# The last chunk of a Mamba block: where its input and its norm's offset are added, and where GpSimd makes the next block's tap matrices

## The chip, the cores and the metric

The kernel runs on one NeuronCore of a Trainium2 chip. The metric is the device time of one execution in microseconds (us); times are the median of the runs shown. The engines are TensorE (PE in the profile, its weight load PEld), VectorE (DVE), ScalarE (ACT), GpSimd (POOL), and SyncE (SP), which here only issues DMAs.

## The reference

The whole network has four layers on an image tensor `x` of 2 x 256 channels x 32 x 32. The change lies in layer 0 and at its border to layer 1. Layer 0 is two Mamba blocks, each with a layer norm and a residual; the second runs over flipped channels, and the input `x` of the network is added to what comes out:

```python
def mamba_block(x, in_w, in_b, conv_w, conv_b, xproj_w, dt_w, dt_b, A_log, Dp, out_w, out_b):
    u = x.reshape(b, L, c)                                  # L = 1024 tokens, c = 256
    xs, res = jnp.split(u @ in_w + in_b, 2, axis=-1)        # 512 inner channels each
    xs = silu(causal_conv4(xs, conv_w) + conv_b)            # per channel, 4 taps
    dt, Bm, Cm = jnp.split(xs @ xproj_w, [16, 32], axis=-1)
    delta = softplus(dt @ dt_w + dt_b)
    A = -jnp.exp(A_log)
    dA  = jnp.exp(delta[..., None] * A)                     # 16 states
    dBu = delta[..., None] * Bm[:, :, None, :] * xs[..., None]
    # over tokens: h = dA * h + dBu ;  y = sum over states of h * C
    y = (ys + xs * Dp) * silu(res)
    return y @ out_w + out_b

xt = xt + layernorm(mamba_block(xt, m1...), ln1_w, ln1_b)
xt = flip(xt)
xt = xt + layernorm(mamba_block(xt, m2...), ln2_w, ln2_b)
# layer 0:  x = x + flip(xt);   layer 1: a dilated 7x7 convolution of x gives attention weights, ...
```

Layers 2 and 3 (attention and experts) follow and are not touched.

## The kernel before

**Tiling.** The activations `x` lie in SBUF as [128 channels, 2 channel chunks, 2 images, 1024 tokens], and `xt` is the same tile seen as [128, 2, 2048]. The Mamba work is cut into eight units: two blocks (`m1`, `m2`) times four chunks of 512 tokens (`TC`). Chunks 0 and 1 are image 0, chunks 2 and 3 are image 1. `xt` is updated in place.

**Three parts of a unit.** `front` makes the projections, the convolution and `delta`, `du`. `scan` runs 16 states; for each state n it loads a row of B to all partitions (`m_b`, line 457), multiplies it with `du` on GpSimd in two halves (the *products*, line 461), makes `exp(delta * A)` on ScalarE (line 468), scans on VectorE in four pieces (line 472), transposes on TensorE (line 440) and accumulates `y` on VectorE (line 449, `scalar_tensor_tensor`, from PSUM). `back` computes the gate, the skip term, the output projection (lines 524 and 528), the norm (`norm_rows`, lines 160 to 168), transposes back (line 179), and then, for each of the two channel chunks `cc`, updates `xt`.

**The update of `xt` in `back`.** Line 540 (ScalarE) makes `r = ps * ln_w + ln_b` from the transposed norm, line 543 (GpSimd) adds `r` to `xt`, and for the second block lines 547 and 548 load the network's input into a tile `m_x` by an SP DMA and add it on GpSimd. The tiles of `r` and of `m_x` share the tag `"r"`, which has three buffers.

**The order.** `layer0` weaves the parts together: `scan` has 63 slots, one at each scan piece, and `paced(63, steps)` calls the steps of other generators in given slots. A tuple `(generator, many, first, end)` spreads `many` steps over the slots `first` to `end`. While unit u is scanned, the front of unit u + 1 and the back of unit u - 1 run in its slots. State n covers slots 4n - 1 to 4n + 2. The tile framework then sets the order in each engine's queue: it takes instructions by the order in which they are written, but lets one go ahead of another that, by its own estimate, isn't ready. [...]

**The tap matrices.** The convolution runs on TensorE with 16 diagonal matrices per block, each the identity scaled by a column of weights on GpSimd (`diagonals`, line 269). Those of `m2` go into the buffer that those of `m1` have held until the last convolution of `m1`, so they are made in unit 2, in slots 26 to 38.

**The last unit.** There, the slots also hold the convolution of layer 1 for the first two row blocks of image 0 (`early`). Five steps of the unit's own `back` (four gate matmuls and the `Silu`) are in its slots; all the rest of it comes after the scan, woven with the convolution of the third row block:

```python
        acc = {2: taps.bank(ps_ht.tile([P, TC], F32, tag="ht", name="early_acc2"))}
        both(taps.convolve(0, pair, acc), done[0], 3)
        taps.read(acc, lg)
```

Then the pools of layer 0 are closed, and `layer1` opens its own in the same memory. Its first work is the loads of the tap pairs (`pair`, line 747, SP), a clearing of the fourth one's second half and of `band` (lines 744 and 852, GpSimd), and `turn`, which copies image 0 on GpSimd (line 863) and transposes it (line 864). Its convolution (line 769, `acc`) then keeps TensorE in work.

Of the kernel before, what the change touches and what calls it, by code (L numbers as in the profile page):

```python
# [10 lines left out]
F32 = mybir.dt.float32  # L11
# [3 lines left out]
ALU = mybir.AluOpType  # L15
# [4 lines left out]
P = 128  # L20
NB = 2
HW = 1024
# [3 lines left out]
NCC = C // P  # L26
NT = T // P
TC = 512
# [3 lines left out]
NDC = DI // P  # L32
# [201 lines left out]
class Mamba:  # L234
# [180 lines left out]
    def scan(self, j, before, between, start=False):  # L415

        net, nc, m, scanp = self.net, self.net.nc, self.m, self.scanp
        xs, bd, ct, delta, du = self.chunks[j]
        state, first = self.state, self.first(j)
        ya = self.two.tile([P, TPC, DI], F32, tag="ya", name=f"{m}_ya_{j}")
        yb = self.one.tile([P, TPC, DI], F32, tag="yb", name=f"{m}_yb_{j}")
        self.chunks[j] = xs, ya, yb
        G = 2
        half = [P, G, TC]

        def keep(n, hs):  # L430
            for g, h in enumerate(hs):
                nc.scalar.copy(state[:, n, g * G : (g + 1) * G], h[:, :, TC - 1])

        def rest(n, hs):


            for i in range(TPC):
                ps = self.ps_ht.tile([P, DI], F32, tag="ht", name=f"{m}_ht_{j}_{n}_{i}")
                for dc in range(NDC):
                    nc.tensor.transpose(  # L440
                        ps[:, dc * P : (dc + 1) * P], hs[dc // G][:, dc % G, i * P : (i + 1) * P],
                        net.ident,
                    )
                yield
                c = ct[:, i, n : n + 1]
                if n in (0, self.ASIDE):
                    nc.scalar.activation((yb if n else ya)[:, i, :], ps, AF.Copy, scale=c)
                else:
                    nc.vector.scalar_tensor_tensor(  # L449
                        ya[:, i, :], ps, c, ya[:, i, :], ALU.mult, ALU.add  # L450
                    )
                if i == 0 and first:
                    keep(n, hs)

        for n in range(NS):
            b = scanp.tile([P, TC], F32, tag="b", name=f"{m}_b_{j}_{n}", bufs=4)
            nc.sync.dma_start(b, bd[n].partition_broadcast(P))
            hs = []
            for g in range(NDC // G):
                h = scanp.tile(half, F32, tag="h", name=f"{m}_h_{j}_{n}_{g}", bufs=6)  # L460
                (nc.vector if start and n == 0 else nc.gpsimd).tensor_mul(  # L461
                    h, du[:, g * G : (g + 1) * G, :], b.unsqueeze(1).to_broadcast(half)
                )
                hs.append(h)
            for dc in range(NDC):
                da = self.ps_da.tile([P, TC], F32, tag="da", name=f"{m}_da_{j}_{n}_{dc}")
                i = dc * NS + n
                nc.scalar.activation(  # L468
                    da, delta[:, dc, :], AF.Exp, scale=self.aneg[:, i : i + 1]
                )  # L470
                h = hs[dc // G][:, dc % G, :]
                nc.vector.tensor_tensor_scan(  # L472
                    h, da, h, 0.0 if first else state[:, n, dc : dc + 1], ALU.mult, ALU.add
                )


                next(before, None)
                if n or dc:
                    next(between, None)
            before = chain(before, rest(n, hs))  # L480
        for _ in between:
            pass
        return before

    def back(self, j):

        net, nc, m, xt = self.net, self.net.nc, self.m, self.xt
        y, *sums = self.chunks.pop(j)
        tok = slice(j * TC, (j + 1) * TC)
        gate = self.one.tile([P, NDC, TC], F32, tag="gate", name=f"{m}_gate_{j}")  # L490
        for dc in range(NDC):
            ps = self.ps_mm.tile([P, TC], F32, tag="mm", name=f"{m}_g_{j}_{dc}")
            for kc in range(NCC):
                nc.tensor.matmul(  # L494
                    ps, lhsT=self.gate_sb[:, kc, dc * P : (dc + 1) * P], rhs=xt[:, kc, tok],
                    start=(kc == 0), stop=(kc == NCC - 1),
                )
            nc.scalar.activation(  # L498
                gate[:, dc, :], ps, AF.Identity, bias=net.col(f"{m}_in_b", NDC + dc)
            )  # L500
            yield
        nc.scalar.activation(gate, gate, AF.Silu)
        yield

        for dc in range(NDC):
            ps = self.ps_mm.tile([P, TC], F32, tag="mm", name=f"{m}_y_{j}_{dc}")
            nc.tensor.matmul(
                ps, lhsT=self.skip[:, dc, :], rhs=y[:, dc, :], start=True, stop=False
            )
            for k, ya in enumerate(sums):  # L510
                for i in range(TPC):
                    nc.tensor.matmul(
                        ps[:, i * P : (i + 1) * P], lhsT=ya[:, i, dc * P : (dc + 1) * P],
                        rhs=net.ident, start=False, stop=(k == 1 and i == TPC - 1),
                    )
            nc.vector.tensor_mul(y[:, dc, :], ps, gate[:, dc, :])
            yield
        o = self.one.tile([P, TPC, C], F32, tag="o", name=f"{m}_o_{j}")
        found = []
        for i in range(TPC):  # L520
            if i % 2 == 0:
                ps = self.ps_mm.tile([P, TC], F32, tag="mm", name=f"{m}_out_{j}_{i}")
            a = ps[:, i % 2 * C : (i % 2 + 1) * C]
            nc.tensor.matmul(
                a, lhsT=net.ones_row, rhs=self.out_b, start=True, stop=False
            )
            for dc in range(NDC):
                nc.tensor.matmul(
                    a, lhsT=y[:, dc, i * P : (i + 1) * P], rhs=self.out_sb[:, dc, :],
                    start=False, stop=(dc == NDC - 1),  # L530
                )
            found.append(a)
            yield
        tiles = [o[:, i, :] for i in range(TPC)]
        net.norm_rows(tiles, found, nc.scalar)
        yield
        for cc in range(NCC):
            ps = net.transposed(self.ps_mm, tiles, cc, "mm")
            r = self.one.tile([P, TC], F32, tag="r", name=f"{m}_r_{j}_{cc}", bufs=3)
            nc.scalar.activation(  # L540
                r, ps, AF.Identity, scale=net.col(f"{m}_ln_w", cc), bias=net.col(f"{m}_ln_b", cc)
            )
            nc.gpsimd.tensor_add(xt[:, cc, tok], xt[:, cc, tok], r)
            if self.x is not None:
                x = self.one.tile([P, TC], F32, tag="r", name=f"{m}_x_{j}_{cc}", bufs=3)
                at = j % (HW // TC) * TC
                nc.sync.dma_start(x, self.x[j // (HW // TC), cc, :, at : at + TC])
                nc.gpsimd.tensor_add(xt[:, cc, tok], xt[:, cc, tok], x)
            yield
# [25 lines left out]
def layer0(net, x, x_dram, m1, m2, load_image, taps, conv_dram, lg):  # L575
# [4 lines left out]
    tc, nc = net.tc, net.nc  # L580
    with (
# [10 lines left out]
        xt = x.rearrange("p c b t -> p c (b t)")  # L592
        pools = (wpool, one, two, scanp, dram, ps_mm, ps_da, ps_ht)
        blocks = [
            Mamba(net, "m1", pools, xt, None, *m1), Mamba(net, "m2", pools, xt, x_dram, *m2)
        ]
# [8 lines left out]
        for m, r in zip(blocks, rows):  # L605
            m.out_b = r
        norm.image(0)
        units = [(m, j) for m in blocks for j in range(NCH)]
        norm.image(1)
        for _ in units[0][0].front(0, alone=True):  # L610
# [3 lines left out]
        for u, (m, j) in enumerate(units):  # L614
            steps = [(b, Mamba.GATED, 0, 35) for b in done]
# [4 lines left out]
                fronts.append(a.front(k))  # L620
            if u == NCH - 2:

                steps.append((blocks[1].diagonals(), NDC * 4, 26, 38))
            rest = m.load_rest() if u and j == 0 else iter(())
            steps += [(f, Mamba.HEAD, 0, 38) for f in fronts]
            steps += [(rest, 1, 37, 38)]
# [2 lines left out]
            if u + 1 < len(units):  # L629
                n = 9 if u else 12  # L630
                steps += [(islice(aside, n), n, 40, 63)]
            else:
# [16 lines left out]
                def early():  # L649
                    for k in range(2):  # L650
                        a = ps_acc.tile([P, TC], F32, tag="acc", name=f"early_acc{k}")
                        acc = {k: taps.bank(a)}
                        yield from taps.convolve(0, pair, acc)
                        taps.read(acc, lg)

                steps += [(early(), 112, 3, 63)]
            own = m.back(j)
            if u + 1 == len(units):

                steps += [(islice(own, 5), 5, 44, 58)]  # L660
            before = m.scan(j, before, paced(63, steps), u == 0)
            done = [own]
        for _ in before:
# [1086 lines left out]
```

## Time and profile before

| what | value |
|---|---|
| runs | 2171.8, 2173.26, 2174.47 us; median 2173.26 us |
| profiled execution, its own time | 2172.59 us |
| its span in the trace | 2170.9 us |
| what lies around the span | 1.69 us |
| PE / PEld busy | 1889.3 us (87%) / 1345.8 us (62%) |
| DVE / ACT / POOL busy | 1402.7 us (65%) / 959.9 us (44%) / 1027.6 us (47%) |
| DVE in 100 to 1000 us | 86.6 to 96.5 us busy of each 100 |
| PE in 1000 to 1200 us | 92.22 and 97.00 us busy of 100 |
| GpSimd products, line 461 | 254 of 2364 ns |
| VectorE scans, line 472 | 512, of 1268 ns with a carried state and 1208 ns without |
| VectorE accumulation from PSUM, line 449 | 448 of 732 ns |
| GpSimd adds of 128 x 512, lines 543 and 548 | 16 of 1268 ns, 8 of 1269 ns |
| GpSimd scalings to tap matrices of 128 x 128, line 269 | 32 of 627 ns |

The time of a group is the sum over its instructions; an engine that is busy for a large share of the whole need not bound every stage. For this change two short stretches matter: around 330 us, where unit 2 is scanned, and 1087 to 1105 us, where layer 0 ends and layer 1 begins.

### The profile page before, as it was taken

To read this page: it belongs to the slowest core of one execution; us is meant where nothing else is said; L and a number is where in the kernel's file an instruction comes from. 1 tells how busy PE (TensorE), PEld (TensorE's weight loads), DVE (VectorE), ACT (ScalarE), POOL (GpSimd) and SP (SyncE) were. 2 spreads that over 40 slices of the span, in tenths; PEclk is the share of its full clock that TensorE was granted. 3 is DMA by queue.
4 is the path that set the end of the run, shared out by engine and by line. 5 is a ranking of instruction groups with operands and counts; after the bars stand their busy time and mean duration, and the time that the engine had idled before them with its cause. 6 is when DMAs were issued, how large, how long until landed. Compare 5 with 4: busy or idle time off the path is not lost.

```text
span 2170.9 us, 27318 instructions
## 1 busy us (share of the span) xinstructions
PE 1889.3 (87%) x9652; PEld 1345.8 (62%) x9652; DVE 1402.7 (65%) x2210; ACT 959.9 (44%) x1611; POOL 1027.6 (47%) x726
## 2 busy tenths in 40 slices
PE   6888798888989879799989989949999699859996
PEld 2364555556555645455656556539999467649995
DVE  6999997999999999897405575652222544442223
ACT  4676776767777767653213454411010132301111
POOL 3796887959698695964225420012332000023331
PEclk8969988897989889899999999969999799979997
DMA  2121121111212111310030100028999200059998
GB/s 107 45 69 40 40 67 35 53 40 45 63 48 60 35 48 34 86 40 20 5 64 1 49 15 10 20 86 304 323 332 333 83 10 10 20 208 320 334 330 294
DMA packets 90499, 223.87 MB, mean 103 GB/s; under 512 B 35467, under 2 KB 51728, under 8 KB 79732
## 3 DMA queue, kind: packets, MB, share of 16 engines
q1 hardware_dynamic: 77636, 198.29, 27.2%
q0 software_dynamic: 7728, 19.15, 3.0%
q10 hardware_dynamic: 4992, 4.59, 0.7%
q8 instruction: 81, 1.33, 0.3%
q14 instruction: 62, 0.51, 0.1%
HBM read 204.60 MB, written 19.37 MB: 103 GB/s over the span
## 4 chain that ended last, share of the span: by engine, by line
PE 32%; DVE 22%; issue 19%; POOL 12%; ACT 9%; DMA 5%; POOLq 0%; SPq 0%; ACTq 0%; DVEq 0%
DVE m_h L472 11%; DVE m_ya L449 5%; PE acc L769 3%; POOL x L1527 3%; POOL l_yd L1577 3%; PE m_ht L440 3%; PE av L1283 3%; POOL m_h L461 3%; PE early_acc L769 2%; PE sc L1257 2%; ACT m_da L468 2%; DMA l_yd<-y,target 2%; PE h L1106 2%; PE w L1115 1%; PE m_xd_ps L351 1%
## 5 line engine op out<-in xcount | busy, mean ns | idle before, releaser
L461 POOL TENSOR_TENSOR m_h<-m_du,m_b 128x1024 f32<-128x1024 f32 x254 | 594.4, 2364 | 227.6 <-PE m_ht L440 126.8
L440 PE MATMUL m_ht<-ident,m_h 128*128 128x128 f32 x2048 | 360.2, 306 | 107.2 <-DVE m_ya L449 78.4
L440 PEld LDWEIGHTS m_ht<-ident,m_h 128*128 128x128 f32 x2048 | 266.2, 156 | 299.0 <-issue 105.2
L468 ACT ACTIVATE m_da<-m_delta,m_aneg 128x512 f32<-128x512 f32 x512 | 349.0, 690 | 219.7 <-DVE m_h L472 218.8
L1527 POOL DMA_INDIRECT x<-l_zd,source x82 | 84.5, 1031 | 569.9 <-DVE source L1472 215.3
L449 DVE SCALAR_TENSOR_TENSOR m_ya<-m_ht,m_ct,m_ya 128x512 f32<-128x512 f32 x448 | 319.3, 732 | 29.2 <-PE m_ht L440 27.8
L472 DVE TENSOR_TENSOR_SCAN m_h<-m_da,m_state,m_h 128x512 f32<-128x512 f32 x256 | 316.8, 1268 | 26.9 <-POOL m_h L461 20.7
L472 DVE TENSOR_TENSOR_SCAN m_h<-m_da,m_h 128x512 f32<-128x512 f32 x256 | 302.8, 1208 | 25.3 <-ACT m_da L468 15.2
L1557 PEld LDWEIGHTS h<-xts,we 128*128 128x128 f32 x2528 | 298.3, 194 | 6.8 <-issue 2.9
L1557 PE MATMUL h<-xts,we 128*128 128x128 f32 x2528 | 299.4, 277 | 1.9 <-issue 1.5
L1564 DVE TENSOR_TENSOR hid<-hid,h 128x512 f32<-128x512 f32 x79 | 54.3, 687 | 255.5 <-PE h L1557 252.0
L1563 ACT ACTIVATE hid<-h 128x512 f32<-128x512 f32 x79 | 47.2, 597 | 381.7 <-issue 299.3
L1571 PE MATMUL o<-we,hid 128*128 128x256 f32 x632 | 150.4, 380 | 2.2 <-DVE y L1576 1.6
L1577 POOL DMA_INDIRECT l_yd<-y,target x79 | 79.0, 1000 | 142.7 <-DVE y L1576 136.4
L1571 PEld LDWEIGHTS o<-we,hid 128*128 128x128 f32 x632 | 113.7, 190 | 15.7 <-DVE y L1576 2.8
L336 PE MATMUL m_conv<-m_pre,m_taps 128*128 128x512 f32 x240 | 114.6, 596 | 6.8 <-ACT m_gate L498 5.6
L769 PE MATMUL early_acc<-x,early 128*98 128x448 f32 (+24 forms) x308 | 100.5, 453 | 0.0
L769 PE MATMUL acc<-x,pair 128*98 128x416 f32 (+21 forms) x308 | 94.0, 452 | 0.0
L1576 DVE COPY y<-o 128x256 f32<-128x256 f32 x79 | 33.6, 425 | 69.3 <-PE o L1571 69.3
L309 PE MATMUL m_in<-x,m_in_sb 128*128 128x512 f32 x128 | 67.7, 653 | 7.6 <-ACT m_pre L313 5.2
L769 PEld LDWEIGHTS acc<-x,pair 128*98 128x98 f32 x308 | 47.6, 167 | 39.1 <-issue 33.6
L494 PE MATMUL m_g<-x,m_gate_sb 128*128 128x512 f32 x128 | 66.5, 633 | 3.9 <-ACT m_o L168 2.1
(318 smaller groups left out, 2849.2 us busy)
## 6 DMA issues: line engine op xcount, KB each, us to landing
we<-in_l_experts_dram SPq DMA_DIRECT2D x82, 1536.0 KB
m_b<-m_bd SPq DMA_DIRECT2D x128, 256.0 KB
w<-in_l_w_dram SPq DMA_DIRECT2D x21, 256.0 KB
l_zd<-l_z SPq DMA_DIRECT2D x7, 512.0 KB
l_yl<-l_yd SPq DMA_DIRECT2D x10, 256.0 KB
l_yl<-l_yd ACTq DMA_DIRECT2D x10, 256.0 KB
early<-taps SPq DMA_DIRECT2D x7, 343.0 KB
pair<-taps SPq DMA_DIRECT2D x7, 343.0 KB
```

The lines of the kernel that those rows point to most:

```text
L309: nc.tensor.matmul(ps, lhsT=self.in_sb[:, kc, mc * P : (mc + 1) * P], rhs=self.xt[:, kc, tok], start=(kc == 0), stop=(kc == NCC - 1),)
L336: nc.tensor.matmul(ps, lhsT=self.taps[:, dc * 4 + k, :], rhs=pre[:, dc, k : k + TC], start=(k == 0), stop=(k == 3),)
L440: nc.tensor.transpose(ps[:, dc * P : (dc + 1) * P], hs[dc // G][:, dc % G, i * P : (i + 1) * P], net.ident,)
L449: nc.vector.scalar_tensor_tensor(ya[:, i, :], ps, c, ya[:, i, :], ALU.mult, ALU.add)
L461: (nc.vector if start and n == 0 else nc.gpsimd).tensor_mul(h, du[:, g * G : (g + 1) * G, :], b.unsqueeze(1).to_broadcast(half))
L468: nc.scalar.activation(da, delta[:, dc, :], AF.Exp, scale=self.aneg[:, i : i + 1])
L472: nc.vector.tensor_tensor_scan(h, da, h, 0.0 if first else state[:, n, dc : dc + 1], ALU.mult, ALU.add)
L769: nc.tensor.matmul(a[:, lo - 16 * k : hi - 16 * k, co : co + n], lhsT=lhsT, rhs=self.x[:, kc, b, lo - r0 : hi - r0, ci : ci + n], start=(u ...
L1527: nc.gpsimd.indirect_dma_start(out=x, out_offset=None, in_=zd[:, :], in_offset=bass.IndirectOffsetOnAxis(ap=source[:, g : g + 1], axis=0), ...
L1557: nc.tensor.matmul(ps[:, at], lhsT=w12[:, s, kc, at], rhs=xt[:, kc * P : (kc + 1) * P], start=(kc == 0), stop=(kc == NCC - 1),)
L1571: nc.tensor.matmul(ps[:, :C], lhsT=ht[:, mc * P : (mc + 1) * P], rhs=w[:, 8 + mc, :], start=(mc == 0), stop=(mc == NHC - 1),)
L1577: nc.gpsimd.indirect_dma_start(out=yd[g], out_offset=bass.IndirectOffsetOnAxis(ap=target[:, g : g + 1], axis=0), in_=y, in_offset=None, bo ...
```

## The change

Three edits. (1) Each scaling that makes a tap matrix of `m2` is traced inside `tc.issue_after(...)`, which puts it in GpSimd's queue behind the last product traced so far (`self.product`, set in `scan`); they are spread from slot 22 rather than 26. (2) In the last unit, two new steps follow the `Silu` of the gate, one for each channel chunk: the input is loaded, the norm's offset `ln_b` is added to it on GpSimd, and the sum is added to `xt` on GpSimd. They are within the scan: the own steps in its slots are now seven over slots 44 to 62, where they were five over 44 to 58. (3) At the end of the last unit, one VectorE instruction for each channel chunk, `ps * ln_w + xt` from PSUM, stands in place of the ScalarE activation, the two GpSimd adds and the load.

```diff
@@ scan
-                (nc.vector if start and n == 0 else nc.gpsimd).tensor_mul(
+                made = (nc.vector if start and n == 0 else nc.gpsimd).tensor_mul(
                     h, du[:, g * G : (g + 1) * G, :], b.unsqueeze(1).to_broadcast(half)
                 )
                 hs.append(h)
+            self.product = made
@@ back
-    def back(self, j):
+    def back(self, j, last=False):
...
         nc.scalar.activation(gate, gate, AF.Silu)
         yield
+        if last:
+            for cc in range(NCC):
+                x = self.one.tile([P, TC], F32, tag="r", name=f"{m}_x_{j}_{cc}", bufs=3)
+                at = j % (HW // TC) * TC
+                nc.sync.dma_start(x, self.x[j // (HW // TC), cc, :, at : at + TC])
+                nc.gpsimd.tensor_scalar_add(x, x, net.col(f"{m}_ln_b", cc))
+                nc.gpsimd.tensor_add(xt[:, cc, tok], xt[:, cc, tok], x)
+                yield
...
         for cc in range(NCC):
             ps = net.transposed(self.ps_mm, tiles, cc, "mm")
+            if last:
+                nc.vector.scalar_tensor_tensor(
+                    xt[:, cc, tok], ps, net.col(f"{m}_ln_w", cc), xt[:, cc, tok],
+                    ALU.mult, ALU.add,
+                )
+                yield
+                continue
             r = self.one.tile([P, TC], F32, tag="r", name=f"{m}_r_{j}_{cc}", bufs=3)
@@ layer0
+        def behind(m, steps):
+            while True:
+                with tc.issue_after(m.product.ins):
+                    if next(steps, steps) is steps:
+                        return
+                yield
...
-                steps.append((blocks[1].diagonals(), NDC * 4, 26, 38))
+                steps.append((behind(m, blocks[1].diagonals()), NDC * 4, 22, 38))
...
-            own = m.back(j)
+            own = m.back(j, u + 1 == len(units))
             if u + 1 == len(units):
-                steps += [(islice(own, 5), 5, 44, 58)]
+                steps += [(islice(own, 7), 7, 44, 62)]
```

## The prediction

> **What bounds the kernel now.** I read the page first, then windows of 100 us, the chain of waits around the two places that the diff touches, and the timeline of each engine there. The page's rows of slices (54.3 us each) show two regimes in layer 0, which ends in slice 21:
>
> ```profile
> span 2170.9 us, 27318 instructions
> PE   6888798888989879799989989949999699859996
> DVE  6999997999999999897405575652222544442223
> ```
>
> VectorE stands at 9 up to about 1000 us, so the scans bound units 0 to 6; from there PE is at 9 and VectorE falls to 4, so the last unit and the convolution after it are PE's. A stall of VectorE before 1000 us, and a hole in PE after it, each cost what they last.
>
> The hole is at the border to layer 1. The chain of waits there (start, us, what):
>
> ```profile
> 1090.28 0.91 ACT m_o L168 x2
> 1091.19 1.93 issue
> 1093.11 0.79 ACT m_r L540
> 1093.97 1.27 POOL x L543
> 1095.26 2.59 DMA m_x<-in_x_dram
> 1097.99 1.27 POOL x L548
> 1099.31 0.68 POOL pair L744
> ```
>
> After the norm there is a row of ScalarE, GpSimd, a load that had to wait for its buffer (three under tag "r"), and GpSimd again. The timeline of the same place shows what else is late, and what is held by it:
>
> ```profile
> 1094.45 0.34 ACT L788 ACTIVATE lg<-early_acc,taps_bias 98x96 f32<-98x96 f32 x1
> 1094.82 0.32 DVE L786 TENSOR_SCALAR lg<-early_acc,taps_bias 98x96 f32<-98x96 f32 x1 [5.60 <-ACT lg L788]
> 1099.27 10.55 SPq L747 DMA_DIRECT2D pair<-taps  x7
> ```
>
> The convolution's last read ends at 1095.14. Layer 1 starts on SP, VectorE and GpSimd together at 1099.3, when the last add to `xt` (to 1099.25) lets layer 0's memory go. PE has no work from 1094.3 to 1101.1. The windows there (length, PE, PEld, DVE, ACT, POOL busy, granted clock, DMA):
>
> ```profile
> 1094.30:1101.10 6.80, 0.00 (x0) 0.00 (x0) 1.83 (x11) 0.49 (x2) 6.43 (x9) 0.79 0.20 51
> 1101.10:1104.70 3.60, 2.88 (x9) 1.48 (x10) 0.00 (x0) 1.28 (x4) 2.17 (x9) 0.50 1.24 212
> 1104.70:1108.90 4.20, 4.20 (x7) 1.66 (x8) 0.00 (x0) 0.21 (x1) 0.45 (x2) 0.55 1.32 191
> 1108.90:1120.00 11.10, 11.10 (x31) 4.75 (x30) 0.00 (x0) 0.00 (x0) 0.00 (x0) 1.00 0.51 74
> ```
>
> The hole also costs clock: PE returns at half speed and has it back at about 1108.9.
>
> The other place is unit 2, GpSimd's and VectorE's timelines:
>
> ```profile
> 324.64 4.67 POOL L461 TENSOR_TENSOR m_h<-m_du,m_b 128x1024 f32<-128x1024 f32 x2 [2.53 <-issue]
> 329.29 9.29 POOL L269 TENSOR_SCALAR m_taps<-ident,cols_sb 128x128 f32<-128x128 f32 x16
> 338.55 4.66 POOL L461 TENSOR_TENSOR m_h<-m_du,m_b 128x1024 f32<-128x1024 f32 x2
> 340.93 2.34 DVE L472 TENSOR_TENSOR_SCAN m_h<-m_da,m_h 128x512 f32<-128x512 f32 x2 [4.84 <-POOL m_h L461]
> ```
>
> The 16 scalings, written one to a slot, run in one burst, since all become ready with the buffer. The next product waits behind them, and VectorE stands 4.84 us, the longest single wait on a product in 100 to 1000 us.
>
> [...] 0.50 and 0.55 after 6.8 us of idleness; a PE wait of 2.06 us at 1033 left the clock at 1.00, one of 3.13 us at 344 is followed by 0.79 in 341 to 352. [...] the same operation in line 449 takes 0.732 us, which I use. [...] no line before scales or shifts 512 elements by a column on GpSimd.
>
> **Part 1, tap matrices behind products.** Nothing is removed; 16 scalings of 0.58 us (9.29 / 16) move. Slot s belongs to state (s + 1) // 4, so slots 22 to 37 put one behind state 5's product, four each behind those of 6, 7 and 8, three behind state 9's. Products come every 7.2 to 8 us (309.59, 317.43, 324.64) and take 4.66, which leaves 2.5 to 3.3 us; four scalings take 2.32, five 2.9. They fit, but barely. The product that stood at 338.55 could then run at 324.64 + 7.9 = 332.5 or behind five scalings at 332.2, with its first half ready at 334.9; VectorE wants it at 336.09. So the wait of 4.84 us goes. Late next is ScalarE: it is in `Silu` and table loads from 332.58 to 337.27, so the second scan of that state can't start before 337.96, 0.7 us after the first ends. Gain at most 4.84 - 0.7 = 4.1. Each later batch can push its product by up to 0.4 us. PE was 9.89 of 12 us busy in that stretch and worked off other things in the wait, which it must now do beside the transposes. Bounds: a gain of 4.8, and a loss of about 2 if the new order in the queues adds a wait like the 3.13 us on PE at 344. I take 3.0. The taps are needed in unit 3, so their lateness is free; no DMA is moved.
>
> **Part 2, the input and offset within the scan.** Added: two loads on SP, two shifts and two adds on GpSimd. An add is 1.27 us. [...] I take 1.6. Sum 2 x 2.9 = 5.7 us, at most 7.3. The cover is GpSimd in the last unit:
>
> ```profile
> 1043.69 4.68 POOL L461 TENSOR_TENSOR m_h<-m_du,m_b 128x1024 f32<-128x1024 f32 x2 [10.68 <-PE m_ht L440]
> 1053.99 1.27 POOL L548 TENSOR_TENSOR x<-x,m_x 128x512 f32<-128x512 f32 x1
> 1087.34 0.24 POOL L125 IOTA iota<- 128x128 f32 x1 [32.08 <-PE m_out L528]
> ```
>
> It waits 10.68 us ahead of the last product and 32 us behind the last add. The adds to `xt` must wait for the gate matmuls (done at 1043.3), so they fall just before, or behind, the last product. On SP the loads stand with the previous chunk's two, and behind them come only small loads at 1087 and layer 1's pairs. One more tenant of tag "r" makes the previous chunk's second load wait for one add more (1050.9 rather than 1049.6), and with the chain's 2.6 us it lands at 1053.5, still ahead of its add at 1053.99. Cost 0; 0.9 us if an add goes just ahead of the last product. Without the cover it would be 5.7.
>
> **Part 3, one VectorE step.** Removed behind the transposes: two activations (1.45 us), four adds (2 x 1.27 + 2 x 1.26) and the wait for a buffer and a load. Added: 2 x 0.73 on VectorE, which is idle there. The transposes end at 1093.0 and 1093.5, so the two steps end by about 1094.6. Late next is the convolution's read, 1095.14, unchanged because PE runs the convolution to 1094.3 whatever stands there. Layer 0's memory goes at 1095.2 in place of 1099.3: **4.1 us**. All that follows (tap pairs 343 KB each, clearing, copies, transposes) hangs on that release, and PE is full from 1104.7 to 1212, so it moves as one. If VectorE's queue has the read ahead of the two steps, they end at 1096.6 and 2.6 remains.
>
> PE's hole becomes 1094.3 to 1097.0, 2.7 us, between the 2.06 that kept the clock and the 3.13 that lost it. Four wide matmuls at 0.85 rather than 0.43 us, and a few short ones, are worth up to 2 us; I take 0.5.
>
> **Sum.** 3.0 + 4.1 + 0.5 = 7.6 us off the profiled 2172.59 (span 2170.9 and 1.69 around it) is 2165.0; the median shown is 0.67 above that execution, so **2165.6**. A measurement can tell about 0.2% (4.3 us) from no change, that is 2168.9 and 2177.6.
>
> **Rivals.**
> *A, both gains* (56 in 100): 2161 to 2168. For it: both waits are in the chain.
> *B, the tail alone* (24): the burst goes, but VectorE then waits for PE or ScalarE, or the new order in the queues puts a like wait elsewhere in units 2 to 6. VectorE already waited there 20.7 us for ScalarE and 17.4 for PE in 100 to 1000. 2173.26 - 4.1 - 0.5 = 2168.7, from 2167 to 2171: on the bound, half of it faster.
> *C, little of either* (10): VectorE's steps come behind the read (2.6), part 1 loses 2: 2172.7. Also here: `issue_after` leaves the burst whole, because the buffer comes free after the later products.
> *D, slower* (10): the new adds stand ahead of the last product in GpSimd's queue. The second's load is on SP behind the previous chunk's second, which waits for an add to end at 1050.9; with its own 2.6 us and the buffer's wait it lands by about 1056, and a shift and an add later the product runs at 1059, not at 1043.7. VectorE wanted it at 1046, so 15 us are lost, less 4.6 at the end and 0 to 3 in unit 2: 2181 to 2184. It decides from a delay of 12 us on. Against it: state 15's product is written ahead of the second step, in slot 59 against 60.
>
> The range takes in A and B and most of C: 2160 to 2173. Faster: 0.53 of A, 0.13 of B, some of the rest: 0.67. Slower: D and a larger mishap of order, 0.11. Same: 0.22.
>
> **What would show it.** Right: scalings in groups of four or five between products around 325 to 355, no wait near 4.8 us; in the last unit shifts and adds between 1040 and 1060 or in the gap behind; `pair` loads some 0.1 us behind the read of the last bank; PE's hole 2.7 us. Wrong: scalings still in a burst or products starting later than their buffers allow; VectorE's steps behind the read; `pair` issued more than 1 us behind it; the last product later against the scan than now.

## The result and the profile after

The changed kernel takes 2166.99 us (median of 20 runs) beside 2175.45 us (20 runs) of the kernel before on the same chip: a ratio of 0.9959 [0.9949, 0.9969], some 9 us faster, interval 6.7 to 11.1. In later runs, which had after and before side by side again, it was 0.9942 [0.9919, 0.9964]. The forecast was 7.6 us less than before, 2165.6 us; the kernel before took 2.2 us more in these 20 runs than in the three that the forecast started from.

The page of after, its first line and the two rows of slices that the prediction read:

```profile
span 2165.4 us, 27316 instructions
PE   6888899897989889799999899949999699859996
DVE  6999999999999999897314575652222544432223
```

VectorE's row has a 9 in the seventh slice (from 325 us on), where a 7 stood before. For a size the rows are too coarse. I measured between landmarks instead, instructions that both kernels have: the start of a given GpSimd product (line 461; they are numbered from 0 here, two for most states, so that product 70 opens state 4 of unit 2 and product 96 state 1 of unit 3), and the first matmul of layer 1's convolution.

| stretch | before | after | after once more |
|---|---|---|---|
| start to product 70 (unit 2, ahead of the scalings) | 309.6 | 312.1 | 309.8 |
| product 70 to 96 (rest of unit 2, into unit 3) | 112.88 | 104.28 | 104.28 |
| product 96 to 246 (units 3 to 6) | 581.4 | 581.8 | 581.4 |
| product 246 to 252 (last unit, states 12 to 14) | 39.80 | 41.49 | 41.50 |
| product 252 to the first `acc` of layer 1 | 61.2 | 56.9 | 56.9 |

The change sits in the second, fourth and fifth row: -8.6, +1.7 and -4.3, together -11.2 us. The first row moved by 2.5 us with the same instructions, and layers 1 to 3 of the profiled after are another 2.8 us longer with the same work; so its span fell by 5.5 us only (2170.9 to 2165.4), that of its second execution by 9.2 (2161.7). A single execution of this kernel doesn't tell 3 us.

**Unit 2.** GpSimd's and VectorE's timelines of after (start, us, instruction, count, and the idle time ahead of it with what ended it):

```profile
327.18 4.67 POOL L461 TENSOR_TENSOR m_h<-m_du,m_b 128x1024 f32<-128x1024 f32 x2 [2.53 <-issue]
331.83 2.92 POOL L269 TENSOR_SCALAR m_taps<-ident,cols_sb 128x128 f32<-128x128 f32 x5
335.02 4.67 POOL L461 TENSOR_TENSOR m_h<-m_du,m_b 128x1024 f32<-128x1024 f32 x2 [0.27 <-issue]
339.67 2.33 POOL L269 TENSOR_SCALAR m_taps<-ident,cols_sb 128x128 f32<-128x128 f32 x4
345.99 4.67 POOL L461 TENSOR_TENSOR m_h<-m_du,m_b 128x1024 f32<-128x1024 f32 x2 [3.99 <-issue]
...
338.55 2.32 DVE L473 TENSOR_TENSOR_SCAN m_h<-m_da,m_h 128x512 f32<-128x512 f32 x2
```

The scalings stand in groups of five, four, four and three behind the products of states 6 to 9; the one that was written behind state 5 came with those of state 6. The product behind five of them starts 7.84 us after the one before it, where the burst had made that 13.9 us. The last line is the pair of scans that had waited 4.84 us; it runs without a wait, and both scans back to back.

VectorE's waits over the whole stretch, first before, then after (engine, tile and line, whom it waited for: us in total, times, the longest):

```profile
DVE m_h L472 <- POOL m_h L461: 6.1, 2, 4.8
DVE m_h L472 <- ACT m_da L468: 4.0, 5, 1.8
DVE m_ya L449 <- PE m_ht L440: 3.9, 5, 1.4
DVE m_xs L516 <- PE m_y L512: 0.7, 1, 0.7
```

```profile
DVE m_h L473 <- ACT m_da L469: 3.6, 5, 1.3
DVE m_ya L449 <- PE m_ht L440: 1.9, 4, 1.1
DVE m_h L473 <- POOL m_h L461: 1.1, 2, 0.6
```

VectorE is busy 97.76 us of this stretch before and 97.58 after: its work is the same, and the stretch is that work plus its waits. These fell from 14.7 to 6.6 us, 8.1 of the 8.6: 5.0 by GpSimd, 2.7 by TensorE, 0.4 by ScalarE. (Each wait is booked under whatever ended it last.)

**The border.** The timeline of after:

```profile
1089.09 1.41 DVE L550 SCALAR_TENSOR_TENSOR x<-mm_t,cols_sb,x 128x512 f32<-128x512 f32 x2 [3.85 <-PE mm_t L179]
1089.64 0.77 POOL L878 MEMSET band<- 128x384 f32 x2 [4.78 <-PE mm_t L179]
1090.45 10.68 SPq L773 DMA_DIRECT2D pair<-taps  x7
1090.72 0.32 DVE L812 TENSOR_SCALAR lg<-early_acc,taps_bias 98x96 f32<-98x96 f32 x1 [0.23 <-ACT lg L814]
...
1096.64 9.82 PE L795 MATMUL acc<-x,pair 128*98 128x512 f32 x19
```

The pair loads go out when the second VectorE step ends, and ahead of the read of the last bank (1090.72 to 1091.04). From the last product to these loads it was 55.58 us before and is 50.74 now: 4.8 us earlier. Windows of after (length, PE, PEld, DVE, ACT, POOL busy, granted clock, DMA share, GB/s):

```profile
1090.30:1091.35 1.05, 0.02 (x2) 0.01 (x1) 0.82 (x5) 0.34 (x1) 1.05 (x4) 1.00 0.03 8
1091.35:1094.35 3.00, 2.37 (x9) 1.13 (x9) 1.04 (x8) 1.25 (x4) 2.24 (x9) 1.00 0.96 178
1094.35:1096.60 2.25, 2.09 (x6) 1.06 (x7) 0.00 (x0) 0.98 (x3) 1.39 (x6) 0.52 1.28 199
1096.60:1101.50 4.90, 4.90 (x7) 1.77 (x7) 0.00 (x0) 0.37 (x1) 0.56 (x2) 0.52 1.32 191
```

TensorE's hole is 1.05 us. Then come transposes in turn with GpSimd's copies (GpSimd is busy 2.24 of 3.00 us, and each waits for the other), 14 of them ahead of `acc` where 9 stood there before. The clock falls all the same, to 0.52 from 1094.35 to 1101.5: 7.15 us, where it was 7.8 us at 0.50 and 0.55.

**The shifts and adds in the scan**, GpSimd's timeline of the last unit:

```profile
1039.71 4.68 POOL L461 TENSOR_TENSOR m_h<-m_du,m_b 128x1024 f32<-128x1024 f32 x2 [12.39 <-PE m_ht L440]
...
1047.49 1.58 POOL L511 TENSOR_SCALAR m_x<-m_x,cols_sb 128x512 f32<-128x512 f32 x1
1049.15 1.27 POOL L512 TENSOR_TENSOR x<-x,m_x 128x512 f32<-128x512 f32 x1
...
1083.37 0.24 POOL L125 IOTA iota<- 128x128 f32 x1 [27.42 <-PE m_out L538]
```

Both, and the second pair at 1053.03 and 1054.68, lie behind the last product; 27.42 us of idle time are still left.

### The profile page after: what moved, and what is told of

Read it like the earlier page. It is cut to its first block, busy times and chain, and to the rows that moved or that the text cites. A ratio compares the mean times of both kernels' runs of the same rounds, so it can differ in the third digit from the quotient of the medians.

```text
span 2165.4 us, 27316 instructions
## 1 busy us (share of the span) xinstructions
PE 1890.4 (87%) x9652; PEld 1343.7 (62%) x9652; DVE 1403.3 (65%) x2212; ACT 957.8 (44%) x1609; POOL 1028.0 (47%) x726
## 4 chain that ended last, share of the span: by engine, by line
PE 30%; issue 17%; DVE 14%; POOL 10%; ACT 7%; DMA 4%; POOLq 0%; ACTq 0%; DVEq 0%
DVE m_h L473 7%; PE acc L795 3%; POOL x L1553 3%; POOL l_yd L1603 3%; DVE m_ya L449 3%; PE av L1309 3%; PE sc L1283 2%; DMA l_yd<-y,target 2%; PE early_acc L795 2%; PE h L1132 2%; PE m_ht L440 2%; ACT m_da L469 2%; POOL m_h L461 2%; PE w L1141 1%; DMA x<-l_zd,source 1%
## 5 line engine op out<-in xcount | busy, mean ns | idle before, releaser
L1553 POOL DMA_INDIRECT x<-l_zd,source x82 | 84.5, 1030 | 571.5 <-DVE source L1498 217.0
```

Of the source, the lines that this page charges most:

```text
L1553: nc.gpsimd.indirect_dma_start(out=x, out_offset=None, in_=zd[:, :], in_offset=bass.IndirectOffsetOnAxis(ap=source[:, g : g + 1], axis=0), ...
```

## The experiments

My theory: the scalings' burst holds VectorE in unit 2, and its split frees it; at the border the release of layer 0's memory moves ahead; the added GpSimd work is covered. The rivals: unit 2's gain comes from elsewhere, or is a matter of single executions; one half of the tail alone is enough; the cover of the added work is thin.

### Each part alone

`e1_taps_only` is after with the last unit's steps as before (`m.back(j)`, five own steps in slots 44 to 58). `e2_tail_only` is after with the scalings as before:

```diff
-                steps.append((behind(m, blocks[1].diagonals()), NDC * 4, 22, 38))
+                steps.append((blocks[1].diagonals(), NDC * 4, 26, 38))
```

> Part 1 alone: the scalings go behind the products, the end of layer 0 is as before. Theory T1 (the burst costs its wait of 4.8 us on VectorE, and what that wait drags along in unit 2: TensorE stuck 3.1 us behind the copy of xd, and then at half clock): 4 to 7 us faster, ratio 0.997 to 0.998; no product wait above 2.5 us, and the stretch from the product before the scalings to the end of unit 2 is shorter by that amount. Theory T2 (the tail makes the whole gain of 8.5 us; VectorE's wait comes back as waits for TensorE or ScalarE): 0 to 1 us, ratio 0.9995 to 1.000.

> Parts 2 and 3 alone: the burst of 16 scalings stays. T1: 4.3 us faster (4 to 5), ratio about 0.998; VectorE waits some 4.8 us for a product in unit 2 as before, and the loads of the pairs are issued when VectorE's second step ends. T2: 7 to 9 us faster, ratio 0.996 to 0.997.

e1: 0.9948 [0.9932, 0.9965], 2168.41 us beside 2177.42. Unit 2's stretch is 104.27, as in after; the border takes 61.1, as before. e2: 0.9964 [0.995, 0.9978], 2171.62 us. Unit 2's stretch is 111.60 and the border 56.9. So each part moves its own stretch; the other's stays, to within 1.3 us. Theory T2, by which the scalings' part is worth nothing, falls. In the times the parts are 11.3 us (7.6 to 14.8) and 7.8 (4.8 to 10.9), both above what T1 forecast (4 to 7, and 4 to 5), the second by no more than its noise. Their sum, 19.1, is above what both together gave: the intervals overlap with that of the later runs (12.6, 7.8 to 17.6) and not with the first one's (6.7 to 11.1). The profile gives 8.6 and 4.3 - 1.7. Of e2's surplus its profile shows 1.3 us in unit 2 and 2.0 in units 3 to 6; why they are there isn't explained.

### After once more

> The kernel after, unchanged, once more beside the partial kernels. If the parts add up as their stretches in the traces say (unit 2 shorter by 8.6 us from the product before the scalings to the twelfth product of unit 3; the end shorter by 4.3 us from the last product to layer 1's first matmul), the time is about 12.9 us below the kernel before, ratio 0.994. If something gives 3 to 4 us back when both are there, it is 8 to 9.5 us, ratio 0.9957 to 0.9963, and a stretch of the trace must show where.

0.9942 [0.9919, 0.9964], some 12.6 us; the stretches are the last column of the table. (What the expectation calls the twelfth product of unit 3 is product 96, its third.) Unit 2, states 12 to 14 and the border repeat to 0.1 us, and the 2.5 us of the first row don't.

### Coarser groups, and none

`e5_groups_of_8` is after with eight scalings behind each of two products. `e6_no_scalings` is before without any: `m2` is convolved with `m1`'s taps, so the values are others and the experts' shares with them, and only unit 2 is read.

```diff
@@ e5
-                    if next(steps, steps) is steps:
-                        return
+                    for _ in range(8):
+                        if next(steps, steps) is steps:
+                            return
...
-                steps.append((behind(m, blocks[1].diagonals()), NDC * 4, 22, 38))
+                steps.append((behind(m, blocks[1].diagonals()), 2, 23, 39))
@@ e6
-                steps.append((blocks[1].diagonals(), NDC * 4, 26, 38))
+                blocks[1].taps = blocks[0].taps
```

> The kernel after, but the scalings in two groups of eight, behind the products of states 6 and 8. Eight take 4.65 us, where GpSimd has 2.5 to 3.3 us of slack. T1 (only what exceeds the slack and VectorE's own reserve of about 1.5 us counts): VectorE waits under 1 us for the product behind each group, and the time is within 2 us of the kernel after, so 7 to 9 us faster than before. A cost in proportion to the size of the group would make each wait about 2.4 us and leave half of part 1's gain: 5 to 6 us faster than before. T2: no difference from the kernel after, and VectorE's waits move without effect.

> The kernel before with no scalings for m2 at all: m2's convolution uses m1's tap matrices, so the second block's values are others, and the experts' groups may differ a little in size; unit 2 is what is read. T1: unit 2 gains as with part 1 alone, within 1.5 us, since groups of four or five fit in GpSimd's slack. If even the groups cost something, this one is over 2 us faster than part 1 alone in unit 2. T2: 0 to 1 us.

e6: unit 2's stretch is 104.09, 0.2 us below after's 104.28. Sixteen scalings in groups of three to five are thus free. (The whole is 1.0052 [1.0037, 1.0068], with its last experts longer.) e5: 0.9967 [0.9953, 0.9981], stretch 109.07, with VectorE's waits

```profile
DVE m_h L473 <- ACT m_da L469: 4.6, 7, 1.8
DVE m_ya L449 <- PE m_ht L440: 4.2, 7, 1.2
DVE m_h L473 <- POOL m_h L461: 3.0, 2, 2.7
```

Eight scalings (4.7 us) don't fit between two products: one wait is 2.7 us, where T1 expected less than 1, and about two fifths of GpSimd's part are back.

### The burst behind other states

Is the loss of 8.6 us tied to the place, and is it a multiple of the wait of 4.84 us? Three kernels are after with all 16 scalings in one burst behind the product of another state:

```diff
-                    if next(steps, steps) is steps:
-                        return
+                    for _ in range(16):
+                        if next(steps, steps) is steps:
+                            return
...
-                steps.append((behind(m, blocks[1].diagonals()), NDC * 4, 22, 38))
+                steps.append((behind(m, blocks[1].diagonals()), 1, 35, 36))   # e9; 27, 28 in e10; 39, 40 in e11
```

> The kernel after, but all 16 scalings in one group behind state 9's product; only GpSimd's order differs. In the kernel before, the burst stands behind state 6's product, VectorE waits 4.8 us and unit 2 is 8.6 us longer than without. If such a wait costs 1.7 to 1.8 times its length wherever it falls, unit 2 is 7 to 10 us longer than in the kernel after. If the surplus came from that place alone (TensorE's wait for the copy of xd just behind it), it is longer by VectorE's wait here and no more, 4 to 5.5 us.

> The same with the group behind state 7's product. Wherever-theory: 7 to 10 us longer in unit 2 than the kernel after; place-theory: 4 to 5.5 us, or more only if TensorE has to wait over 2.5 us here too and its clock falls below 0.9 in the 28 us that follow.

> The same with the group behind state 10's product. Wherever-theory: 7 to 10 us longer in unit 2 than the kernel after; place-theory: 4 to 5.5 us, or more only with a TensorE wait over 2.5 us and a lower clock behind it.

e9: 0.995 [0.9932, 0.9968]; e10: 0.9958 [0.9945, 0.997]; e11: 0.9979 [0.9968, 0.9989]. The stretch of unit 2 is 107.95, 107.67 and 113.73. Set out as VectorE's busy time and its waits, with the other kernels' (us):

| kernel | stretch | busy | waits by GpSimd | by TensorE | by ScalarE |
|---|---|---|---|---|---|
| before (e3 the same) | 112.88 | 97.8 | 6.1 | 4.6 | 4.0 |
| e2, before's order here | 111.60 | 96.7 | 6.5 | 4.2 | 3.8 |
| e4, before's order here | 109.64 | 97.6 | 5.3 | 2.3 | 4.0 |
| after | 104.28 | 97.6 | 1.1 | 1.9 | 3.6 |
| after once more | 104.28 | 97.5 | 2.1 | 1.7 | 2.9 |
| e1, after's order | 104.27 | 97.5 | 1.5 | 1.7 | 3.5 |
| e7, after's order | 106.70 | 97.0 | 0.4 | 4.5 | 4.5 |
| e6, no scalings | 104.09 | 97.7 | 0.6 | 2.1 | 3.7 |
| e5, groups of 8 | 109.07 | 97.0 | 3.0 | 4.2 | 4.6 |
| e9 | 107.95 | 97.0 | 7.7 | 2.2 | 1.0 |
| e10 | 107.67 | 97.1 | 6.2 | 2.6 | 1.8 |
| e11 | 113.73 | 97.9 | 6.5 | 6.2 | 2.7 |

With a burst, wherever it stands, VectorE waits 5.3 to 7.7 us for GpSimd in this stretch, with the split 0.4 to 2.1, and without scalings 0.6. So this part goes with the burst: GpSimd ran the group where it had been put (in e9 9.31 us behind state 9's product), and the next product behind it. Not all of it stands right behind the group: in e10 the burst ends at 349.19, VectorE's wait there is 2.84 us, and the other 3.4 us fall after 406 us, in unit 3's first states, where no run tells what they hang on.

The stretch is not longer by GpSimd's part alone. In e9 the waits by GpSimd are 6.6 us above after's and those by ScalarE 2.7 below, so that it is 3.7 us longer; e10 is 3.4 us longer and e11 9.5. Neither theory holds: 7 to 10 us wherever the burst stands came in e11 alone, and 4 to 5.5 us in none. There is no fixed multiple of the longest wait, either.

The part by TensorE runs from 1.7 to 6.2 and doesn't follow the order of the scalings alone: e4 has before's order and 2.3, e7 after's and 4.5. Over four profiled executions of each order, before's takes 109.6 to 112.9 us (mean 111.8) and after's 104.3 to 106.7 (mean 104.9). So the 8.6 us are the far end of a range that begins at 2.9, with a mean of 6.9.

In e11 the burst does it without one long wait; VectorE's waits there are

```profile
DVE m_h L473 <- POOL m_h L461: 6.5, 5, 1.9
DVE m_ya L449 <- PE m_ht L440: 6.2, 6, 2.3
DVE m_h L473 <- ACT m_da L469: 2.7, 3, 1.8
```

In these executions of one order the clock differs. The windows 43 to 57 us behind product 70, after first and then e7, with the same order of scalings in GpSimd's queue:

```profile
355.14:369.14 14.00, 13.91 (x81) 10.04 (x80) 13.77 (x17) 11.01 (x15) 10.98 (x8) 0.93 0.16 34
```

```profile
356.00:370.00 14.00, 12.52 (x50) 8.32 (x49) 11.81 (x14) 10.93 (x15) 9.81 (x8) 0.70 0.07 22
```

At 0.70 TensorE did 50 matmuls where it did 81 at 0.93, and VectorE was busy for 2.0 us less. Before, the three windows from 29 to 71 us had 0.81, 0.87 and 0.71, and e4 0.88, 0.93 and 0.83, with a stretch 3.2 us shorter.

The traces also say when the granted clock changes. In each of the 14 traces all stretches of lowered clock start on one grid with a step of 3.413 us, to within 4 ns, and it is not tied to the program: from the start of the span its first point stands at 2.17 us in after and at 2.81 in its second execution. In before and in after the granted clock is 0.50 in each of these stretches and 1.00 outside them. Counted from the start of product 70, a grid point stands at 0.20 to 0.64 us in after, its second execution and e1, and the clock first falls at 41.2 to 41.6 us, for one step; in e7 the point stands at 0.95 us, and the clock falls at 48.7, for three steps. In before and e3 it stands at 0.16 to 0.18 us and the clock falls at 37.7 for two steps, in e4 at 0.29 us and it falls at 37.8 for one. The four engines run the same instructions in the same order within each group, so where the grid lies is the one difference found. No run sets it, and the rule by which a step lowers the clock is not worked out here.

### Filling TensorE's wait

Does the burst cost the clock? Before has a TensorE wait of 3.1 us there, ahead of the transposes `m_ct_ps`, and after has none. `e8_filled_wait` is before with eight filler matmuls in its place:

```diff
+        if m == "m1" and j == 3:
+            for _ in range(8):
+                nc.tensor.matmul(ps, lhsT=net.ident, rhs=xs[:, 0, :], start=True, stop=True)
```

> The kernel before, burst and VectorE's wait of 4.8 us included, with eight matmuls of 128 x 512 (3.4 us at full clock, their result is overwritten) put on TensorE just ahead of the transposes that wait 3.1 us for ScalarE's copy of xd in unit 2. If the loss of the burst above its wait comes from the clock that TensorE loses in that wait, the clock stays near 1.00 in the 30 us that follow and the stretch from the product before the scalings to the twelfth product of unit 3 falls from 112.9 us by 2 to 4 us. If the loss is in the order of the queues alone, the stretch stays at 112 to 114 us.

It was slower: 1.0018 [1.0007, 1.0029], stretch 116.80, with waits of 9.8 us by GpSimd and 8.3 by TensorE. TensorE's timeline:

```profile
348.49 8.83 PE L365 MATMUL m_ct_ps<-m_xs,ident 128*128 128x512 f32 x16 [3.26 <-DVE m_xs L519]
```

The filler itself waited 3.26 us, and with 8.83 us, where I had estimated 3.4 at full clock, it was longer than the hole. The clock was 0.88, 1.00 and 0.88, better than before's, and the stretch 3.9 us longer all the same. The test failed, since the wait was not filled. What speaks for a cost in clock is an agreement only: in before, e2, e3 and e4, which have the 3.1 us wait, the clock falls 36.3 to 37.8 us behind product 70, at the last grid point before that wait ends, and in after, its second execution, e1, e6 and e7, which don't have it, not before 41.2.

### Half of the tail

`e3_input_early` adds the input within the scan but leaves the norm's weight and offset to ScalarE and GpSimd at the end. `e4_add_late` has the VectorE step, and GpSimd adds input and offset behind it. Both have the scalings as before.

```diff
@@ e3, within the scan
+                nc.gpsimd.tensor_add(xt[:, cc, tok], xt[:, cc, tok], x)
@@ e4, behind the VectorE step
+                nc.gpsimd.tensor_add(xt[:, cc, tok], xt[:, cc, tok], shifted[cc])
```

> The burst of scalings stays. The input is added within the scan, but offset and weight stay in ScalarE's step and GpSimd's add behind the norm. Theory of the end as a chain: the two loads and the two last adds go (the last add of the norm then ends at 1096.45 on the old time axis, not at 1099.25), so layer 1 starts 2.8 us earlier and 1.5 to 2 us later than with the whole of parts 2 and 3. Rival: the gain of 4.3 us comes from the VectorE step alone, because the load was fast enough: then 0 to 1 us here.

> The burst of scalings stays. The input is loaded and the offset added to it within the scan, VectorE's step stands behind the norm, but the sum is added to the activations on GpSimd behind that step. Chain theory: VectorE's steps end 0.7 us apart, two adds of 1.27 us follow, so layer 1 starts about 2 us later than with the whole of parts 2 and 3 and 2.5 us earlier than before. Rival (the VectorE step is all that counts): 4.3 us as with both parts.

e3: 0.9993 [0.9981, 1.0004], e4: 0.999 [0.998, 1.0]: no change that can be told. In the profile the border takes 59.6 and 59.5 us, 1.6 and 1.7 below before's 61.2, where both together take 4.3 off. The timelines, e3 first:

```profile
1094.40 2.48 POOL L552 TENSOR_TENSOR x<-x,m_r 128x512 f32<-128x512 f32 x2 [5.15 <-ACT m_r L549]
1096.90 10.95 SPq L765 DMA_DIRECT2D pair<-taps  x7
```

```profile
1090.66 1.41 DVE L551 SCALAR_TENSOR_TENSOR x<-mm_t,cols_sb,x 128x512 f32<-128x512 f32 x2 [3.84 <-PE mm_t L179]
1091.49 2.48 POOL L555 TENSOR_TENSOR x<-x,m_x 128x512 f32<-128x512 f32 x2 [5.07 <-DVE x L551]
1094.00 11.31 SPq L775 DMA_DIRECT2D pair<-taps  x7
```

In both the loads follow the second GpSimd add at once. From the last product they come after 52.8 and 52.7 us, against 55.58 before and 50.74 in after: 2.8 and 2.9 us earlier and some 2 us later, as the chain theory said, so the VectorE step is not all that counts. Of these 2.8 us only 1.6 arrive at `acc`. In each, one pair of GpSimd adds (2.48 us) still stands between the norm and the release.

### More GpSimd work in the scan

`e7_more_in_scan` is after with eight more multiplications by one at the place of the shifts:

```diff
+                for _ in range(4):
+                    nc.gpsimd.tensor_scalar_mul(x, x, net.one)
```

> The kernel after with eight more GpSimd instructions in the last unit: four multiplications by one of each loaded input tile, 1.6 us each, 12.6 us in all, between the shift and the add. Theory (GpSimd is idle there for 27 us behind its last add, and nothing waits for the sum before the norm): no change against the kernel after, the last product starts no later and VectorE's two steps still wait for TensorE's transposes. Rival (the work in the scan is at the edge of its cover): the last product or VectorE's steps are late, and up to 12 us are lost.

0.9941 [0.992, 0.9963]. GpSimd's timeline, with the extra work and the idle time behind it:

```profile
1053.74 6.54 POOL L513 TENSOR_SCALAR m_x<-m_x,one 128x512 f32<-128x512 f32 x4
...
1065.83 6.54 POOL L513 TENSOR_SCALAR m_x<-m_x,one 128x512 f32<-128x512 f32 x4
...
1087.94 0.24 POOL L125 IOTA iota<- 128x128 f32 x1 [14.22 <-PE m_out L540]
```

Another 13.1 us of GpSimd work moved nothing: states 12 to 14 take 41.50 and the border 56.9, as in after. The cover takes this on top of the 5.7 us that the change adds.

## Why the prediction was right, and where it wasn't

**Part 1 (3.0, at most 4.1; measured 8.6, and 6.9 in the mean of four executions each).** The mechanism was right and the size too small. The 4.84 us went, as did a second wait of 1.2 us that I had not counted (6.1 us in two waits). The 0.7 us that I took off for ScalarE didn't come: the two scans run back to back. So the waits by GpSimd fell by 5.0 us here. The rest, 2.7 by TensorE and 0.4 by ScalarE, I had bounded from the wrong side: I feared that TensorE would have to do its work beside the transposes, and it waits less. This rest varies between executions of one order (e7: none of it), with where the clock's grid lies. How much of it the burst causes stays open. Groups of five cost nothing that can be told (e6), so the fit that I called bare is enough; eight are too many (e5).

**Part 2 (0; measured 0).** A shift takes 1.58 us; the 1.6 was an estimate of mine, which no trace of before could show. An add takes 1.27; the sum of 5.7 us is covered, and so are another 13.1 (e7). Rival D, with an add ahead of the last product, did not occur: both adds stand behind it.

**Part 3 (4.1, with 0.5 for the clock; measured 4.3).** The sum is right, two steps in it are not. I let the release of the memory wait for the last bank's read; the loads went out 0.6 us before that read ended, with the VectorE step. The step itself ended where the forecast had it, 50.8 us behind the last product (forecast 50.9); the release goes with it and is 4.8 us earlier, not 4.1. And the hole of 2.7 us became 1.05, by the release and because the clearing of `band` now runs ahead of it, yet it bought hardly any clock: the transposes behind it come in turn with GpSimd's copies, and the clock falls during them, for about as long as before (7.15 us beside 7.8). So the sum came out near because two errors offset each other: the release gave 0.7 us more than forecast, and between it and `acc` 0.5 us were lost where 0.5 were to be gained. The clock fell to 0.52 here behind a hole of 1.05 us and a stretch in which TensorE was busy for 2.37 of 3.00 us. That the hole's length alone would set what it costs in clock was my assumption, which the traces don't show.

**What I had not in the sum: +1.7 us in the profiled execution.** I wrote that a TensorE wait of 2.06 us had kept the clock, and set the hole between it and one of 3.13 us, as if the length of a wait decided. It kept it in the kernel before. The same wait in before and in after:

```profile
1035.06 3.70 PE L494 MATMUL m_g<-x,m_gate_sb 128*128 128x512 f32 x8 [2.06 <-ACT m_o L168]
```

```profile
1029.39 5.40 PE L496 MATMUL m_g<-x,m_gate_sb 128*128 128x512 f32 x8 [2.06 <-ACT m_o L168]
```

Eight equal matmuls take 5.40 us behind it in after, its second execution, e2, e5 and e7, and 3.70 in before, e1, e3, e4, e6, e8, e9, e10 and e11. The last three have the tail of after, so the tail alone doesn't make the loss. In the 25 us ahead of the wait TensorE's busy time is the same in all 14, to within 0.01 us. What differs is where the wait lies on the clock's grid of 3.413 us. Windows of TensorE cut at grid points (length, PE busy, granted clock, DMA share, GB/s), after first and then before:

```profile
1026.17:1029.58 3.41, 1.35 (x7) 1.00 0.00 0
1029.58:1032.99 3.41, 3.41 (x5) 0.50 0.00 0
```

```profile
1029.98:1033.40 3.42, 3.02 (x13) 1.00 0.00 0
1033.40:1036.81 3.41, 1.75 (x4) 1.00 0.00 0
```

In after the wait lies whole in one step, and the clock is halved for the next step; in before a grid point falls within the wait, and it stays. So it is in all: in the five that lose, a grid point stands 0.09 to 0.20 us behind the wait's end, and in the nine others one falls 0.17 to 1.89 us before it, within the wait. The grid lies differently in the two executions of after (its first point at 2.17 and at 2.81 us). So this loss hangs on where the grid lies, and not on the work. Both executions of after lost, and no run shows how often one does. TensorE's busy share of a step doesn't tell it either: at the border of after it was busy 2.46 of the 3.41 us ahead of the fall (1091.02 to 1094.43), more than the 1.75 of before here, which kept the clock. Which share of which work keeps it stays open.

**The total** was 7.6 forecast and 8.9 measured, with rival A, both gains, the one that happened. That it came so near is in part luck: part 1 is mis-sized by more than half. In the profiled execution the clock at 1030 us took 1.7 us back; how many of the 20 runs lose them isn't known.

## What to carry to other kernels

Small independent instructions that all become ready at one moment can run as a burst, and a product behind them comes late (here 16 scalings in 9.29 us, and a wait of 4.84 us on VectorE): put them in groups that fit between the instructions that others wait for, and check the fit against the gap (here up to 2.9 us of scalings in a gap of 2.5 to 3.3 us was free, and 4.7 was not). To cost a stall, set the stage out as the bounding engine's busy time and its waits by releaser; one wait in a timeline is less than the account. At a border where memory changes hands, look for the instruction that ends last on that memory: half of the shortening moved the release by 2.8 of 4.8 us, and the work behind it by 1.6 of 4.3. And before a clock loss of a few us is put down to a change, take a second profile: it can depend on where the clock's grid lies in that execution (here 1.7 us, lost in five of 14 traces).

## What the hardware showed that I had not expected

- Every fall of the granted clock starts on a grid of 3.413 us (14 traces, to within 4 ns) that is not tied to the program. A TensorE wait of 2.06 us left the clock at 1.00 in the nine traces in which a grid point fell within it, and halved it for 3.41 us in the five in which none did; eight matmuls behind it then took 1.7 us more, with the same work ahead.
- On GpSimd an operation with one input of 128 x 512 fp32 and a column takes longer (1.58 us) than an add of two such inputs (1.27 us); a multiplication by a constant column took 6.54 / 4 = 1.64 us.
- Executions of one instruction order differ by 2.4 and 3.3 us in a stretch of 104 to 113 us that VectorE bounds, with the same work on every engine and another course of TensorE's clock.
